# Attention, the last group of four heads: all four scores of a turn in one round, in seven PSUM banks

## The chip, the cores and the metric

The kernel runs on one core of a Trainium2 chip. The metric is the device time of one execution in microseconds (us), and the time of a kernel is the median of its runs. A core has engines that run side by side, each through its own list of instructions in order: PE (TensorE, matrix products), ACT (ScalarE), DVE (VectorE), POOL (GpSimd), and SP, which here only issues DMAs. Semaphores tie them together. PE writes its products into PSUM, eight banks of 128 partitions by 512 float32; ACT and DVE read them from there.

## What is computed

The program is a network of eight layers over x, 4 batches of 1024 tokens by 128 features in float32, each layer adding to x a function of the layer norm of x. Two of the eight are softmax attention, and both are written by one function, so that the change is in both. Cut to what matters:

```python
# L2: 8 heads of 16 features
scores = einsum('bhsd,bhtd->bhst', q, k) / sqrt(dk)
att    = einsum('bhst,bhtd->bhsd', softmax(scores), v)

# L3: 16 heads of 8 features, keys in blocks of 64
exp_scores = exp(scores - m_new)
l_new   = chunk_sum * corr + chunk_sum
out_new = out * corr + einsum('bhqk,bhkd->bhqd', exp_scores, V_blk)
...       # at the end out / l
```

For each head the kernel finds the largest score of each query (the maxima), then the exponentials of the scores less that maximum, then their product with the values.

## The kernel before, in words

`attention` (line 1116) works through groups of four heads of one batch: M = 8 groups in L2 and 16 in L3. The four heads of a group lie on partitions 0, 32, 64 and 96 of a q and a k tile, so that a product over one head's features takes 32 rows of PE's array, and the four heads have four different strips of rows.

The outer loop (line 1397) counts turns, 16 for a group. In turn t one group is scanned (its maxima are found) while the group before it is weighed (its exponentials are taken). A turn has two rounds:

- `scan` (line 1254) takes a PSUM tile of two banks, tag "pa", from a ring of two such tiles: four banks in all. `score` (line 1263) writes two heads' scores into it with two matmuls (line 1265), and one reduction on DVE takes both heads' maxima (line 1273 or 1277).
- `weigh` (line 1310) is called twice in a round, for one head each time: it takes one bank, tag "sm", from a ring of three, writes the head's scores of 128 keys by 512 queries with one matmul (line 1319), and one exponential on ACT (line 1323) reads the bank and writes a quarter of the SBUF tile es.
- `gather` (line 1325) multiplies es with the values: four matmuls (line 1341), one for each head, each taking 32 columns of the array, into the one bank of tag "po". It runs over half of the 512 queries at a time: in round 0 of turn t the second half of turn t-2, in round 1 the first half of turn t-1. Where a new stretch of 512 queries begins (each eighth turn), the first half is passed over and the next round does all 512 columns; after eight turns DVE copies the bank out (line 1348).
- Other steps hang on a turn and round through `at` (line 1353) and are emitted behind the round's own work: `negate` (line 1224), which turns the maxima over and sends them through DRAM into a row of q, `spread`, `value` and `project`, which prepare the next group or batch, and `collect` (line 1356) with the steps of `finish`.

The schedule is written by hand (line 1178): each engine gets its instructions in the order in which the loop emits them. A PSUM tile that is taken anew can be written once all that used its slot before is done.

In the first group there is only scanning (`scan_alone`, line 1281). In the last group there is only weighing: turns M*16 to M*16+15. There the loop before still emits two rounds: heads 2 and 3, a gather, heads 0 and 1, a gather. The "pa" tiles aren't used there: no later group is scanned or projected, and the steps of `finish` that take one come before this stretch or behind it. `negate` of the last group's second half of queries falls into round 1 of its first turn, `collect` of the group before into its second, and the layer norm's sums of three batches (`ln_sums`, line 128, on DVE) into its fourth, seventh and tenth.

Of the kernel before, what the change touches and what calls it, by code (L numbers as in the profile page):

```python
# [9 lines left out]
F32 = mybir.dt.float32  # L10
AF = mybir.ActivationFunctionType
# [4 lines left out]
P = 128  # L16
# [11 lines left out]
class Net:  # L28
# [1087 lines left out]
    def attention(self, H, HD, scale, weights, prepare, finish, last=False):  # L1116
# [13 lines left out]
        nc, tc = self.nc, self.tc  # L1130
        G = H // 4
        W = 32 * H
        M = NB * G
        TURNS = 2 * TPB
        NBM = 9 if last else 2
        wq, wk, wv = weights
        with ExitStack() as c:
# [4 lines left out]
            sm = c.enter_context(tc.tile_pool(name="ats", bufs=3, space=PSUM))  # L1142
# [8 lines left out]
                cp, lhsT=ones.rearrange("p a b -> p (a b)"), rhs=self.ones[0:1, 0:1], start=True, stop=True  # L1151
# [28 lines left out]
            def pair(name):  # L1180
                return pap.tile([P, 2, 512], F32, tag="pa", name=name).rearrange("p a b -> p (a b)")
# [72 lines left out]
            def scan(m, turn, hp):  # L1254


                st = state[m]
                i, n = turn // 2, turn % 2
                if "bm" not in st:
                    st["bm"] = [two.tile([P, 4, 4, NBM], F32, tag=f"bm{h}", name=f"bm{h}") for h in range(2)]  # L1260
                pa = pair("pa").rearrange("p (a b) -> p a b", a=2)

                def score(j):
                    r = slice(32 * j, 32 * j + 32)
                    nc.tensor.matmul(  # L1265
                        pa[:, j % 2, :], lhsT=st["q"][r, i * P : (i + 1) * P],
                        rhs=st["k"][r, n * 512 : (n + 1) * 512], start=True, stop=True,
                    )

                def reduce():  # L1270
                    out = st["bm"][i // 4][:, i % 4, 2 * hp : 2 * hp + 2, :]
                    if last and n == 1:
                        nc.vector.tensor_reduce(  # L1273
                            out[:, :, 1:9], pa.rearrange("p j (c s) -> p j c s", c=8), axis=AX.X, op=ALU.max
                        )
                    else:
                        nc.vector.tensor_reduce(out[:, :, n : n + 1], pa, axis=AX.X, op=ALU.max)  # L1277

                return score, reduce

            def scan_alone(m, turn):


                st = state[m]
                i, n = turn // 2, turn % 2
                if n == 0:
                    both = [scan(m, turn, hp) for hp in range(2)]
                    for j in range(4):
                        both[j // 2][0](j)
                    for _, reduce in both:  # L1290
                        reduce()
                    return
                banks = [sm.tile([P, 512], F32, tag="sm", name="pb") for _ in range(3)]
                banks.append(pop.tile([P, 512], F32, tag="po", name="pb"))
                for j in range(4):
                    r = slice(32 * j, 32 * j + 32)
                    nc.tensor.matmul(
                        banks[j], lhsT=st["q"][r, i * P : (i + 1) * P],
                        rhs=st["k"][r, n * 512 : (n + 1) * 512], start=True, stop=True,
                    )  # L1300
                for j in range(4):
                    out = st["bm"][i // 4][:, i % 4, j, :]
                    if last:
                        nc.vector.tensor_reduce(  # L1304
                            out[:, 1:9], banks[j].rearrange("p (c s) -> p c s", c=8), axis=AX.X, op=ALU.max
                        )
                    else:
                        nc.vector.tensor_reduce(out[:, n : n + 1], banks[j], axis=AX.X, op=ALU.max)  # L1308

            def weigh(m, turn, j):  # L1310

                st = state[m]
                n, kc = turn // TPB, turn % TPB
                es = st.setdefault("es", {})
                if turn not in es:
                    es[turn] = two.tile([P, 4, 512], F32, tag="es", name="es", bufs=5)
                pb = sm.tile([P, 512], F32, tag="sm", name="pb")
                r = slice(32 * j, 32 * j + 32)
                nc.tensor.matmul(  # L1319
                    pb, lhsT=st["k"][r, kc * P : (kc + 1) * P], rhs=st["q"][r, n * 512 : (n + 1) * 512],  # L1320
                    start=True, stop=True,
                )
                nc.scalar.activation(es[turn][:, j, :], pb, AF.Exp, scale=scale)  # L1323

            def gather(m, turn, half):


                st = state[m]
                b, g = m // G, m % G
                n, kc = turn // TPB, turn % TPB  # L1330
                if kc == 0:
                    if half == 0:
                        return
                    st["po"] = pop.tile([P, 512], F32, tag="po", name="po")
                    if n == 0:
                        st["oT"] = two.tile([P, SEQ], F32, tag="oT", name="oT")
                es, po = st["es"][turn], st["po"]
                cols = slice(0, 512) if kc == 0 else slice(256 * half, 256 * half + 256)
                for j in range(4):
                    r = slice(32 * j, 32 * j + 32)  # L1340
                    nc.tensor.matmul(  # L1341
                        po[r, cols], lhsT=vring[b % 2][:, kc, 4 * g + j, :], rhs=es[:, j, cols],
                        start=kc == 0, stop=True, skip_group_check=True,
                    )
                if half == 1:
                    del st["es"][turn]
                    if kc == TPB - 1:
                        nc.vector.tensor_copy(st["oT"][:, n * 512 : (n + 1) * 512], po)  # L1348
# [22 lines left out]
            for b in range(NB):  # L1371

                t = b * G * TURNS
# [5 lines left out]
            for m in range(M):  # L1379
                t = m * TURNS  # L1380
# [15 lines left out]
            t = 0  # L1396
            while t < (M + 1) * TURNS or jobs:
                scans, weighs = TURNS <= t < M * TURNS, TURNS <= t < (M + 1) * TURNS
                if t < TURNS:
                    scan_alone(0, t)  # L1400
                for rnd in range(2):

                    other = 2 - 2 * rnd
                    if scans:
                        score, reduce = scan(t // TURNS, t % TURNS, rnd)
                    if weighs:
                        weigh(t // TURNS - 1, t % TURNS, other)
                    if scans:
                        for j in range(2):
                            score(2 * rnd + j)  # L1410
                        reduce()
                    if weighs:
                        weigh(t // TURNS - 1, t % TURNS, other + 1)

                    w, half = (t - 2, 1) if rnd == 0 else (t - 1, 0)
                    if TURNS <= w < (M + 1) * TURNS:
                        gather(w // TURNS - 1, w % TURNS, half)
                    for what, args in jobs.pop((t, rnd), ()):
                        what(*args)
                t += 1  # L1420
# [405 lines left out]
```

## Time and profile before

| | us |
|---|---|
| median of 3 runs | 2668.34 |
| lowest and highest of the 3 | 2666.43, 2669.78 |
| the profiled execution | 2665.29 |
| its span in the trace | 2663.6 |
| PE busy | 2417.5 (91% of the span) |
| DVE busy | 1795.2 (67%) |
| ACT busy | 1501.7 (56%) |
| first and last exponential of line 1323 | 1014.1, 2529.6 |

The trace of one execution gives each instruction's start and length on its engine. "Busy" of PE says that matmuls are in flight, not that the array works at its peak. A float32 matmul has two records of PE in this trace: line 1319 has 3072 records for 1536 exponentials. "PEld" is the load of the stationary operand, which goes ahead of the matmul. "Idle before" an instruction is the time in which its engine had nothing to do, with what ended it. The chain of waits is followed back from the last instruction: each step is what released the next. PEclk is the share of PE's clock pulses that the chip granted.

### The profile page before, as it was taken

What the parts mean: (1) busy time and instruction counts of PE and PEld (TensorE: products, weight loads), DVE (VectorE), ACT (ScalarE), POOL (GpSimd) and SP (SyncE); (2) the same over time, 40 slices, a digit from 0 to 9 for tenths busy, and PEclk for the clock granted to TensorE, in tenths of its full rate; (3) what the DMA queues carried; (4) which work ended last, traced back from release to release, by engine and by line L of the source; (5) the groups of instructions that cost most, each with busy time, mean ns of one, the idle gap of its engine ahead of it and who ended that gap; (6) DMA issues with size and microseconds to landing.
All of it is one profiled execution on the core that took longest, in us unless ns stands there. A gap on an engine that the chain in (4) does not pass through costs nothing.

```text
span 2663.6 us, 51041 instructions
## 1 busy us (share of the span) xinstructions
PE 2417.5 (91%) x19913; PEld 1222.1 (46%) x19913; DVE 1795.2 (67%) x3670; ACT 1501.7 (56%) x3333; POOL 293.0 (11%) x525
## 2 busy tenths in 40 slices
PE   5687758899997979999999779999999999999968
PEld 3455535699995333333333443333333333333356
DVE  5888877476764767776774357767767776777233
ACT  4466468455554434665566635666666566666632
POOL 6012021000002530000000440000000000000011
PEclk8699879899997989999999879999999999999969
DMA  1333320000000001001000000000000000000000
GB/s 45 74 77 74 73 74 1 1 1 1 1 1 2 1 9 18 14 15 18 14 14 6 5 5 10 9 10 8 8 9 12 8 9 10 8 8 8 3 18 18
DMA packets 116719, 46.66 MB, mean 18 GB/s; under 512 B 88473, under 2 KB 111097, under 8 KB 116474
## 3 DMA queue, kind: packets, MB, share of 16 engines
q1 hardware_dynamic: 116474, 43.35, 8.2%
q8 instruction: 159, 2.61, 0.4%
q14 instruction: 86, 0.70, 0.1%
HBM read 17.04 MB, written 12.98 MB: 11 GB/s over the span
## 4 chain that ended last, share of the span: by engine, by line
PE 57%; DVE 4%; ACT 1%; POOL 1%; issue 1%; SPq 0%; DMA 0%; POOLq 0%; DVEq 0%; ACTq 0%
PE pb L1319 32%; PE po L1341 16%; PE pa L1265 2%; DVE bm L1277 1%; PE pp L1205 1%; PE pv L1186 1%; DVE bm L1304 1%; PE tp L158 1%; PE gp L1014 1%; PE rp L1743 1%; DVE bm L1308 0%; PE pr L1598 0%; PE rp L1520 0%; PE ph L1756 0%; POOL sg L1753 0%
## 5 line engine op out<-in xcount | busy, mean ns | idle before, releaser
L1323 ACT ACTIVATE es<-pb 128x512 f32<-128x512 f32 x1536 | 836.3, 594 | 536.1 <-PE pb L1319 381.8
L1319 PE MATMUL pb<-q,k 32*128 32x512 f32 x3072 | 956.5, 641 | 3.9 <-DVE bm L1308 1.7
L1265 PE MATMUL pa<-k,q 32*128 32x512 f32 x2944 | 846.0, 650 | 10.4 <-DMA q<-q 10.3
L1277 DVE TENSOR_REDUCE bm<-pa 128x2 f32<-128x1024 f32 x496 | 605.0, 1225 | 261.1 <-PE pb L1319 168.0
L1341 PE MATMUL po<-es,v 128*32 128x256 f32 (+1 forms) x5760 | 480.0, 405 | 0.0
L1319 PEld LDWEIGHTS pb<-q,k 32*128 32x128 f32 x3072 | 313.5, 183 | 350.7 <-ACT es L1323 189.8
L1341 PEld LDWEIGHTS po<-es,v 128*32 128x32 f32 x5760 | 114.2, 108 | 543.1 <-issue 508.2
L1273 DVE TENSOR_REDUCE bm<-pa 128x16 f32<-128x1024 f32 x240 | 293.2, 1222 | 97.3 <-PE pb L1319 60.7
L1265 PEld LDWEIGHTS pa<-k,q 32*128 32x128 f32 x2944 | 234.4, 186 | 37.0 <-issue 18.6
L152 POOL TENSOR_SCALAR xn<-x,rs,nm 128x128 f32<-128x128 f32 x112 | 50.3, 464 | 1204.6 <-DVE nm L125 1026.9
L366 DVE TENSOR_TENSOR pr<-T,L 128x31 f32<-128x31 f32 (+15 forms) x248 | 92.0, 371 | 28.0 <-DMA L<-ld 20.7
L369 DVE TENSOR_TENSOR T<-T,pr 128x31 f32<-128x31 f32 (+15 forms) x248 | 93.1, 375 | 8.5
L1348 DVE COPY oT<-po 128x512 f32<-128x512 f32 x48 | 32.8, 682 | 95.6 <-PE po L1341 95.6
L158 PE MATMUL tp<-ident,xn 128*128 128x128 f32 x224 | 47.0, 361 | 42.7 <-ACT xn L154 38.1
L821 ACT ACTIVATE w<-tr,half 128x128 f32<-128x128 f32 x128 | 47.1, 368 | 48.3 <-PE tr L819 45.6
L796 ACT ACTIVATE a<-hp,wb 128x128 f32<-128x128 f32 x128 | 47.1, 368 | 41.6 <-PE hp L792 40.1
L1081 PE MATMUL ep<-L_ffn_expert_w,xnT 128*128 128x512 f32 x128 | 66.8, 654 | 3.3 <-DVE x L1090 3.1
L324 PE MATMUL wide<-bt,kt 32*128 32x128 f32 x512 | 29.9, 360 | 43.9 <-DVE mt L413 31.7
L486 PE MATMUL sp<-ux,kn 128*128 128x256 f32 x128 | 46.1, 493 | 17.7 <-ACT ux L475 17.7
L158 PEld LDWEIGHTS tp<-ident,xn 128*128 128x128 f32 x224 | 33.9, 179 | 61.2 <-ACT xn L154 47.0
L804 DVE TENSOR_TENSOR dlt<-gr,mask 128x128 f32<-128x128 f32 x96 | 28.0, 292 | 48.3 <-PE gr L802 48.3
L853 ACT COPY dr<-tr 128x128 f32<-128x128 f32 x128 | 34.1, 266 | 43.1 <-PE tr L851 41.1
(466 smaller groups left out, 3598.8 us busy)
## 6 DMA issues: line engine op xcount, KB each, us to landing
ld<-kk SPq DMA_DIRECT2D x128, 32.0 KB
L<-ld SPq DMA_DIRECT2D x8, 512.0 KB
td<-T SPq DMA_DIRECT2D x8, 512.0 KB
tb<-td SPq DMA_DIRECT2D x128, 32.0 KB
md<-nt SPq DMA_DIRECT2D x192, 2.0 KB
q<-md SPq DMA_DIRECT2D x192, 2.0 KB
x<-in_L_attn_x_dram SPq DMA_DIRECT2D x4, 512.0 KB
od<-o SPq DMA_DIRECT2D x32, 64.0 KB
```

The costliest lines, as they stand in the source:

```text
L152: nc.gpsimd.tensor_scalar(xn[:, i, :], src[:, i, :], sl, bl, ALU.mult, ALU.add)
L158: nc.tensor.transpose(tp[:, i, :], xn[:, 4 * n + i, :], self.ident)
L366: nc.vector.tensor_mul(pv, T[:, 0 : j + 1, j : j + 1].to_broadcast(sh), L[:, j : j + 1, j + 1 :].to_broadcast(sh))
L369: nc.vector.tensor_sub(T[:, 0 : j + 1, j + 1 :], T[:, 0 : j + 1, j + 1 :], pv)
L796: nc.scalar.activation(self.a, self.hp, AF.Silu, bias=B1)
L1081: nc.tensor.matmul(ep.rearrange("p a b -> p (a b)"), lhsT=self.tok(t), rhs=ew[:, 4 * h : 4 * h + 4, :].rearrange("p a b -> p (a b)"), star ...
L1265: nc.tensor.matmul(pa[:, j % 2, :], lhsT=st["q"][r, i * P : (i + 1) * P], rhs=st["k"][r, n * 512 : (n + 1) * 512], start=True, stop=True,)
L1273: nc.vector.tensor_reduce(out[:, :, 1:9], pa.rearrange("p j (c s) -> p j c s", c=8), axis=AX.X, op=ALU.max)
L1277: nc.vector.tensor_reduce(out[:, :, n : n + 1], pa, axis=AX.X, op=ALU.max)
L1319: nc.tensor.matmul(pb, lhsT=st["k"][r, kc * P : (kc + 1) * P], rhs=st["q"][r, n * 512 : (n + 1) * 512], start=True, stop=True,)
L1323: nc.scalar.activation(es[turn][:, j, :], pb, AF.Exp, scale=scale)
L1341: nc.tensor.matmul(po[r, cols], lhsT=vring[b % 2][:, kc, 4 * g + j, :], rhs=es[:, j, cols], start=kc == 0, stop=True, skip_group_check=True,)
```

## The change

`weigh` takes a list of heads and a function that gives it banks. It takes all banks of the list, then emits the matmuls of all heads, then their exponentials. While a group is scanned, it is called as before: one head, a bank of tag "sm". In the last group it is called once in a turn, in round 0, for all four heads, and round 1 has only its gather and the steps that hang on it. The banks come there from `any_bank`: whenever its list is empty it takes two "pa" tiles, which give two banks each, and three "sm" banks, and it hands these seven out in that order.

```diff
-            def weigh(m, turn, j):
+            def weigh(m, turn, js, bank):
...
-                pb = sm.tile([P, 512], F32, tag="sm", name="pb")
-                r = slice(32 * j, 32 * j + 32)
-                nc.tensor.matmul(
-                    pb, lhsT=st["k"][r, kc * P : (kc + 1) * P], rhs=st["q"][r, n * 512 : (n + 1) * 512],
-                    start=True, stop=True,
-                )
-                nc.scalar.activation(es[turn][:, j, :], pb, AF.Exp, scale=scale)
+                pbs = [bank() for _ in js]
+                for j, pb in zip(js, pbs):
+                    r = slice(32 * j, 32 * j + 32)
+                    nc.tensor.matmul(
+                        pb, lhsT=st["k"][r, kc * P : (kc + 1) * P], rhs=st["q"][r, n * 512 : (n + 1) * 512],
+                        start=True, stop=True,
+                    )
+                for j, pb in zip(js, pbs):
+                    nc.scalar.activation(es[turn][:, j, :], pb, AF.Exp, scale=scale)
+
+            def bank():
+                return sm.tile([P, 512], F32, tag="sm", name="pb")
+
+            spare = []
+
+            def any_bank():
+
+                if not spare:
+                    for _ in range(2):
+                        pa = pair("pe")
+                        spare.extend(pa[:, i * 512 : i * 512 + 512] for i in range(2))
+                    spare.extend(bank() for _ in range(3))
+                return spare.pop(0)
...
-                    if weighs:
-                        weigh(t // TURNS - 1, t % TURNS, other)
+                    if weighs and scans:
+                        weigh(t // TURNS - 1, t % TURNS, (other,), bank)
+                    elif weighs and rnd == 0:
+                        weigh(M - 1, t % TURNS, range(4), any_bank)
...
-                    if weighs:
-                        weigh(t // TURNS - 1, t % TURNS, other + 1)
+                    if weighs and scans:
+                        weigh(t // TURNS - 1, t % TURNS, (other + 1,), bank)
```

## The prediction

> **What bounds the kernel now.** I read first the chain of waits, by line. It names PE, and PE in attention:
>
> ```profile
> PE pb L1319 32%; PE po L1341 16%; PE pa L1265 2%; DVE bm L1277 1%; PE pp L1205 1%; PE pv L1186 1%; DVE bm L1304 1%; PE tp L158 1%; PE gp L1014 1%; PE rp L1743 1%; DVE bm L1308 0%; PE pr L1598 0%; PE rp L1520 0%; PE ph L1756 0%; POOL sg L1753 0%
> ```
>
> Only the last group changes, so I read that stretch alone. The chain in order of time, L3 (start, length, what):
>
> ```profile
> 2473.42 0.57 PE po L1341 x8
> 2473.99 1.22 PE pb L1319 x4
> 2475.20 0.57 PE po L1341 x8
> 2475.77 1.07 PE pb L1319 x4
> 2476.84 0.57 PE po L1341 x8
> ...
> 2480.31 0.59 ACT es L1323
> ...
> 2482.06 1.00 PE po L1341 x8
> 2483.05 1.06 PE pb L1319 x4
> ```
>
> The reader is to see that nothing but PE stands there: scores of two heads (1.07 or 1.22), a gather (0.57), over and over. Two rounds make a turn of 3.43 us. The gather that begins a stretch of 512 queries does 512 columns and takes 1.00, so 256 columns more cost 0.43 and 0.14 of each gather is fixed (changing from row strips to column strips and back). The 1.22 rounds are those in which the second head's bank was released late. L2's stretch shows the same numbers.
>
> Then the last full round of scanning just before, in the timeline (start, length, engine, line, what):
>
> ```profile
> 2472.28 0.69 PE L1319 MATMUL pb<-q,k 32*128 32x512 f32 x1
> 2472.28 0.70 PE L1265 MATMUL pa<-k,q 32*128 32x512 f32 x2
> 2472.30 1.10 PE L1319 MATMUL pb<-q,k 32*128 32x512 f32 x2
> ...
> 2472.82 0.59 PE L1265 MATMUL pa<-k,q 32*128 32x512 f32 x2
> 2472.83 0.59 PE L1319 MATMUL pb<-q,k 32*128 32x512 f32 x1
> ...
> 2473.35 0.64 PE L1341 MATMUL po<-es,v 128*32 128x256 f32 x8
> 2473.43 1.08 ACT L1323 ACTIVATE es<-pb 128x512 f32<-128x512 f32 x2 [0.70 <-PE pb L1319]
> 2473.52 1.23 DVE L1273 TENSOR_REDUCE bm<-pa 128x16 f32<-128x1024 f32 x1 [0.56 <-PE pb L1319]
> ...
> 2480.29 1.57 ACT L1323 ACTIVATE es<-pb 128x512 f32<-128x512 f32 x3 [0.70 <-PE pb L1319]
> ```
>
> Four heads, one on each strip of rows, begin at 2472.28 and the gather follows at 2473.35: 1.07 us, what two heads cost in the last group. Their exponentials begin 1.15 after the scores. The last group thus uses half of the array's strips in the same time. The same stretch by windows:
>
> ```profile
> 2474.00:2529.00 55.00, 54.63 (x360) 17.06 (x360) 9.51 (x46) 34.28 (x65) 0.00 (x0) 1.00 0.03 4
> ```
>
> PE is busy for 54.63 of 55 us, DVE 9.51, ACT 34.28, with the clock granted in full: ACT has a third of the time free.
>
> **The change, part by part.** The stretch runs from the first score of the last group (2473.92) to the copy of the last product (2531.39): 57.47 us. In L2 it is 1423.77 to 1481.24, 57.47 too. No instruction is added or removed: 64 score matmuls, 64 exponentials and all gathers stay; they move.
>
> *A turn on PE.* Scores of four heads once: 1.06. Two gathers in a row: their columns equal those of the 512-column gather, 1.00. Sum 2.06 instead of 3.43. Is PE's list fast enough? A turn issues 24 weight loads with their matmuls. At the end of the stretch 14 loads pass in 0.58 us, so 24 need 1.0; covered.
>
> *A turn on ACT.* Three exponentials in 1.57 with one at 0.60: the next starts 0.485 after the one before. Four: 1.94 a turn, 0.12 under PE. Here the Trainium skill speaks against the change: "TensorEngine Tiling (Array Packing)", section PSUM Bottleneck, says that tiling speeds up the matmuls but not the emptying of PSUM, which may then bound. And "ScalarE: Activation LUTs", section What ACT_TABLE_LOAD costs, prices an ACTIVATE with immediates at 186 ns + 0.833 ns an element and lets neighbours overlap by 93 ns: 612 - 93 = 519 ns each, estimated 2.08 a turn, so that ACT would bound by 0.02. The row gives 0.485, and I take it; by the page the total would be some 0.8 us worse over both layers. Either way the two engines nearly meet: little more is to be had from PE here. From above, with no overlap, an exponential costs 0.60 and the turn 2.40 (a rival below).
>
> *Does PE wait for ACT?* The gather of turn t-1 stands behind the scores of turn t and needs the exponentials of t-1. Those end 1.15 + 3 x 0.485 + 0.60 = 3.21 after their scores began, so 1.15 after the scores of t began; the gather comes at 1.06 + 0.43 = 1.49. No wait, 0.3 to spare.
>
> *Banks.* Seven banks, four a turn: the fourth head of a turn takes a bank used one turn before. If it is an "sm" bank, its exponential was the first of that turn and ended at 1.15 + 0.60 = 1.75, plus 0.06 (the trace's step from an exponential's end to the next load on PE): before 2.06. If it opens a "pa" tile, I take it that both halves must be read first; where these are the first two heads of the turn before, that is 0.485 later, 2.29, and the head starts 0.23 late. Counting the order of the seven through 16 turns gives four such turns, and two of 0.18 behind a turn with one gather less: 1.3 us. Queued behind a late head are the gathers, so it counts in full.
>
> *First turn.* Its third head takes the "pa" tile that DVE's last reduction reads until 2474.75, 0.89 with the 0.06 after 2473.92. This wait is new, and before nothing stood there. Turn 0: 0.89 + 2.06 = 2.95. `negate` hangs on DVE and keeps its place.
>
> *The end.* From the last scores: 3.21 to the end of the exponentials, 0.06, then both halves' products to the copy, 1.12 (the last chain before ran 2530.27 to 2531.39): 4.39.
>
> *Sum.* 2.95 + 14 x 2.06 + 1.3 + 4.39 = 37.5 us instead of 57.5: 20.0 us for each layer, 40.0 for both.
>
> *What was hidden and might show.* The DVE copy of the group before: before, it ended 1.40 after its gather began (2478.56 to 2479.96), and the next gather into that bank now comes 0.57 + 1.06 = 1.63 after; covered by 0.2, and with the cover gone it costs that difference twice in a layer. The maxima of the second half reach q through SP: the last issue ends at 2480.74, and turn 8 begins at 2473.92 + 2.95 + 7 x 2.06 = 2491.3; the longest q transfer on the chain is 2.33, so covered by 8. `ln_sums` and `negate`: DVE works 9.5 us of 37. The work behind the stretch (output DMAs on SP, transposes, layer norm) hangs on the last copy and shifts whole. SP is past the earlier DMAs at 2486 and idle until the end.
>
> *Against the time.* The profiled execution took 2665.3 (span 2663.6); less 40.0 it is 2625.3. The median of the runs is 3.0 above it, so I forecast 2628.
>
> **The rivals.**
>
> - *The two halves of a "pa" tile are tied together*: the matmul into the second half waits until the first half has been read. Within a turn this costs nothing, as all four matmuls precede the exponentials. Four times in 16 turns a tile straddles two turns, and then the next scores wait for all exponentials: 3.27 instead of 2.06, 1.2 each, 4.8 a layer: 2638. For: no row shows a tile read half by half. Against: they are separate banks, and the two score matmuls of one tile show no wait for each other. Chance 0.08.
> - *ACT becomes the bound*: exponentials in a long row at 0.60, a turn of 2.40. 0.34 x 15, less the bank waits it swallows, plus 0.35 at the end: 4.1 a layer, 2636. For: the skill's page, halfway. Against: 1.57 for three. Chance 0.06.
> - *The four don't run side by side*: two pairs, 2.12 + 1.00 = 3.12 a turn, 0.31 x 15 + 0.7 at the end saved: 2658. Against: the scan round, with the same strips, shapes and banks of the same two tags. Chance 0.03.
> - *The other side: the clock.* A turn streams 1.72 us and has 0.34 fixed; at a granted clock c it takes 1.72/c + 0.34, and passes 3.43 below c = 0.56. At 0.50, which windows from 2539 on show behind the attention, the turn is 3.78, the stretch 63.7 and the kernel 2681. For: PE's clock does fall there. Against: it falls where PE was idle for 5 us, and scanning with four strips has 1.00. Waits can't do it: even if scores waited for all exponentials of the turn before, a turn would be 3.27, still under 3.43. Chance 0.03.
>
> **How the numbers follow.** The forecast has 0.78; around it, 0.1 us a turn either way is 3 us for both layers, and runs of one kernel differ by 3.4. The range 2620 to 2638 takes in the first two rivals, and leaves out the third, the fourth and mishaps. From no change I can tell 0.2%, 5.3 us: all but the clock are faster by more. Faster 0.95, same 0.02, slower 0.03.
>
> **What would show it.** In the changed trace's last group: eight score records starting together on four strips, about 1.06 before the gather; 16 gather matmuls in a row; turns of 2.06, of which six last some 0.2 longer; ACT busy for over nine tenths; the stretch 37.5 long in both layers. I am wrong if score rounds stay at two a turn, if PE waits for ACT at each turn, if the exponentials' spacing is over 0.5, or if PEclk falls there.

## The result, and the profile after

| | before | changed |
|---|---|---|
| median of the runs, us | 2669.06 (4 runs) | 2637.38 (4 runs, 2633.47 to 2647.7) |
| ratio to before, 95% interval | | 0.989 [0.9868, 0.9911] |
| the stretch of the last group in L2, us | 57.47 | 42.00 |
| the same in L3 | 57.47 | 42.00 |

The stretch is, as in the prediction, from the last group's first score to its last copy: 1424.76 to 1466.76 in L2, 2459.94 to 2501.94 in L3. It gained 15.5 us a layer where 20.0 were forecast; 30.9 in both, and the medians differ by 31.7.

The profiled execution has a span of 2638.0, only 25.6 under that of before. The other 5.3 us are not in the two stretches: 3.9 of them lie behind the last copy, the rest ahead of the two. Behind the copy the same work met another clock. By windows, first a row of before, then the same part of the changed kernel (stretch, length, PE, PEld, DVE, ACT and POOL busy, PEclk, DMA share, GB/s):

```profile
2601.40:2621.40 20.00, 17.52 (x132) 13.88 (x131) 10.97 (x19) 6.03 (x13) 3.34 (x5) 0.97 0.10 27
```

```profile
2571.90:2591.90 20.00, 17.99 (x104) 13.77 (x103) 10.21 (x17) 4.74 (x10) 2.87 (x4) 0.72 0.10 27
```

At 0.72 PE got through 104 matmuls in the 20 us in which it did 132 at 0.97. From the last copy to the end it is 136.1 us here and 132.2 before; in the traces of the runs below it is anything from 130.5 to 136.0. So I compare stretches, and medians over runs, not spans of two traces.

The chain of waits in L3's last group, in order of time, as shown of before (start, length, what):

```profile
2460.01 1.94 PE pe L1320 x8
2461.95 1.00 PE po L1357 x16
2462.95 0.64 PE pb L1320 x3
...
2464.10 2.07 ACT es L1325 x4
2466.17 0.04 issue
2466.22 0.70 PE pe L1320 x3
...
2467.36 1.43 PE po L1357 x16
2468.78 0.63 PE pb L1320 x2
...
2472.02 4.13 ACT es L1325 x8
2476.15 0.04 issue
2476.19 0.69 PE pe L1320
...
2477.33 1.00 PE po L1357 x16
2478.33 1.14 PE pe L1320 x8
...
2479.50 4.13 ACT es L1325 x8
2483.63 0.04 issue
2483.67 0.69 PE pe L1320
```

What was forecast is there: one score round a turn, both gathers in one row of 16 matmuls (1.00), the first turn's wait (1.94 for the scores, the turn 2.94), four exponentials in 2.07. What is new: ACT stands on the chain. Before the scores of turns 2, 6 and 9 (and 13, behind this cut) PE waits until every exponential of the turn before is done: the last ends at 2466.17 and the scores start at 2466.22. Each time the matmul that waits writes a "pe" bank, a half of a "pa" tile. The windows say the same in sum:

```profile
2462.90:2499.00 36.10, 31.73 (x336) 11.40 (x336) 7.91 (x41) 29.51 (x59) 0.00 (x0) 1.00 0.04 6
```

PE is busy for 31.73 of 36.10 us at the full clock; it stands still for 4.4, and ACT isn't full either. Where the wait sits can be read from the built program's list of PE's instructions (shortened), with the semaphore that each waits for:

```
L1320 Matmult pb_25995<-q0,k0 128x512
L1320 Matmult pb_25996<-q0,k0 128x512
L1320 Matmult pb_25997<-q0,k0 128x512
L1320 Matmult pe_26030<-q0,k0 128x512 [waits Activation]
L1357 Matmult po_25828<-es_25964,v1 32x256 x4
L1320 Matmult pe_26030<-q0,k0 128x512 [waits Activation]
```

This is turn 1 and the start of turn 2. The tile pe_26030 is shared: its first half goes to the last head of turn 1, its second half to the first head of turn 2. The second half is a bank that nobody has used since the tile was taken, yet its matmul waits for ACT. The count that it waits for is the one that the exponential of turn 1's last head raises, the reader of the first half. The built program puts the tile into banks 0 and 1, so the two halves share no bank. (The matmul into the first half waits as forecast, for both exponentials that read the tile's place before.)

### The profile page after: what moved, and what is told of

It reads as the page before. It is cut to its first block, busy times and chain, and to the rows that moved or that the text cites. A ratio compares the mean times of both kernels' runs of the same rounds, so it can differ in the third digit from the quotient of the medians.

```text
span 2638.0 us, 51055 instructions
## 1 busy us (share of the span) xinstructions
PE 2384.1 (90%) x19913; PEld 1216.0 (46%) x19913; DVE 1793.4 (68%) x3670; ACT 1497.1 (57%) x3333; POOL 291.6 (11%) x525
## 4 chain that ended last, share of the span: by engine, by line
PE 55%; DVE 4%; ACT 2%; POOL 1%; issue 1%; SPq 0%; DMA 0%; POOLq 0%; DVEq 0%; ACTq 0%
PE pb L1320 30%; PE po L1357 16%; PE pa L1265 2%; DVE bm L1277 1%; ACT es L1325 1%; PE pp L1205 1%; PE pe L1320 1%; DVE bm L1304 1%; PE pv L1186 1%; PE tp L158 1%; PE rp L1762 1%; PE gp L1014 1%; DVE bm L1308 0%; PE pr L1617 0%; PE kp L1530 0%
## 5 line engine op out<-in xcount | busy, mean ns | idle before, releaser
L1325 ACT ACTIVATE es<-pb 128x512 f32<-128x512 f32 x1462 | 795.7, 595 | 496.1 <-PE pb L1320 339.3
L1320 PE MATMUL pb<-q,k 32*128 32x512 f32 x2924 | 905.8, 640 | 3.2 <-DVE bm L1308 1.7
L1320 PEld LDWEIGHTS pb<-q,k 32*128 32x128 f32 x2924 | 295.3, 183 | 325.7 <-ACT es L1325 170.4
L324 PE MATMUL wide<-bt,kt 32*128 32x128 f32 x512 | 30.4, 365 | 43.0 <-DVE mt L413 30.9
```

The lines of the kernel that those rows point to most:

```text
L1320: nc.tensor.matmul(pb, lhsT=st["k"][r, kc * P : (kc + 1) * P], rhs=st["q"][r, n * 512 : (n + 1) * 512], start=True, stop=True,)
```

## The experiments

Two theories. **Tie**: the program treats a "pa" tile as one thing, so that a matmul into its second half waits until the first half has been read; four turns of 16 begin with such a half. **Supply**: seven banks are too few for four a turn, with ACT this full, whichever way they are dealt out. Each experiment computes the whole function. The edits of the first and of the last experiment are shown against the changed kernel, those of the three between them against the first. The runs of before with which the first four are compared have a median of 2666.31.

**No tile shared by two turns.** The same banks, two "sm" and one whole "pa" tile a turn:

```diff
                 if not spare:
-                    for _ in range(2):
-                        pa = pair("pe")
-                        spare.extend(pa[:, i * 512 : i * 512 + 512] for i in range(2))
-                    spare.extend(bank() for _ in range(3))
+                    spare.extend(bank() for _ in range(2))
+                    pa = pair("pe")
+                    spare.extend(pa[:, i * 512 : i * 512 + 512] for i in range(2))
```

> The same change, the same seven banks, but each turn takes two 'sm' banks for heads 0 and 1 and one whole 'pa' tile for heads 2 and 3, so that no 'pa' tile is shared by two turns. Tie theory (a matmul into the second half of a 'pa' tile waits until the first half has been read): the stalls before the scores of turns 2, 6, 9 and 13 go (1.7 + 3 x 0.98 = 4.6 us a layer), as do the late fourth heads and most of the wait in the first turn; the last group's stretch, first score to last copy, takes 35.7 us a layer instead of 42.0, and the kernel some 2625. Supply theory (seven banks are too few for four a turn with ACT this full, whichever way they are dealt out): the stretch stays at 42 or above, the kernel at 2637.

Measured: 2625.45 (2616.14 to 2626.08, 5 runs), ratio to before 0.9834 [0.9808, 0.986]; the stretch 36.19 us in both layers. The chain in its L3 stretch, and a window of it:

```profile
2467.67 0.63 PE pb L1320 x2
2468.30 0.01 PE pe L1320 x2
2468.31 0.41 PE pb L1320 x2
2468.72 0.01 PE pe L1320 x2
2468.74 1.00 PE po L1356 x16
2469.74 0.63 PE pb L1320 x2
```

```profile
2454.00:2486.00 32.00, 32.00 (x357) 11.19 (x360) 8.29 (x44) 31.04 (x62) 0.00 (x0) 1.00 0.04 7
```

ACT is off the chain, a turn is 2.07 (2467.67 to 2469.74), PE is busy throughout and ACT for 31.04 of 32. No bank was added. Supply falls.

**The tie in every turn.** The same deal, one head later:

```diff
-            spare = []
+            spare, spares = [], []
...
-                    spare.extend(bank() for _ in range(2))
+                    spare.extend(bank() for _ in range(2 if spares else 3))
                     pa = pair("pe")
                     spare.extend(pa[:, i * 512 : i * 512 + 512] for i in range(2))
+                    spares.append(1)
```

> As e1_aligned, but dealt out one head later: the first turn takes three 'sm' banks and the first half of a 'pa' tile, and from then on each turn begins with the second half of the tile of the turn before, then two 'sm' banks, then the first half of the next tile. Banks, matmuls and exponentials are those of e1_aligned, only every turn now shares a tile with the next. Tie theory: every turn waits for all exponentials of the turn before, 3.27 us a turn, the stretch 53 us a layer, the kernel some 2660. Supply theory: no different from e1_aligned; with late heads by bank alone the stretch would be 38 us.

Measured: 2659.86 (20 runs), ratio 0.9974 [0.9966, 0.9983]; the stretch 53.5 us. The chain, L3:

```profile
2474.54 2.05 ACT es L1325 x4
2476.60 0.04 issue
2476.64 0.69 PE pe L1320
...
2477.82 2.06 ACT es L1325 x4
2479.87 0.04 issue
2479.92 0.69 PE pe L1320
```

PE and ACT take turns: a turn is 3.28 (2476.64 to 2479.92), 3.27 by the sum. Between this kernel and the one before it nothing differs but the head at which the deal begins, and that is 17 us a layer. This is the strongest evidence for the tie: the same instructions, the same banks.

**The order within a turn.** No tile is shared, but the tile goes first:

```diff
-                    spare.extend(bank() for _ in range(2))
                     pa = pair("pe")
                     spare.extend(pa[:, i * 512 : i * 512 + 512] for i in range(2))
+                    spare.extend(bank() for _ in range(2))
```

> As e1_aligned, no tile shared between turns, but the 'pa' tile goes to heads 0 and 1 and the 'sm' banks to heads 2 and 3. What a bank waits for is then a later exponential: the fourth head takes the 'sm' bank that the third head had a turn before, read as the third of four, 1.15 + 2 x 0.485 + 0.60 + 0.06 = 2.78 after the scores began, 0.7 later than a turn of 2.06. Tie theory with release by order: every other turn 2.77, the stretch 41 us a layer, the kernel some 2636, though no tile straddles. Supply theory: the same as e1_aligned.

Measured: 2637.87 (4 runs), ratio 0.9884 [0.9857, 0.9911]; the stretch 41.9 us, just what the changed kernel takes, for another reason. The chain, L3:

```profile
2470.47 0.63 PE pe L1320 x2
2471.10 0.01 PE pb L1320
2471.11 0.42 PE pe L1320 x2
2471.53 0.78 PE pb L1320 x3
2472.31 1.00 PE po L1356 x16
2473.31 0.63 PE pe L1320 x2
...
2475.39 0.63 PE pe L1320 x2
```

Here the last head's "pb" comes 0.78 late every other turn: 2.84 and 2.08 us a turn (2470.47, 2473.31, 2475.39). A bank comes free in the order in which its exponential stands among the four: with the same banks and no tile shared, the order alone costs 5.7 us a layer (41.9 against 36.19).

**Two heads at a time with enough banks.** The loop of before, on the banks of the first experiment:

```diff
-                    elif weighs and rnd == 0:
-                        weigh(M - 1, t % TURNS, range(4), any_bank)
+                    elif weighs:
+                        weigh(M - 1, t % TURNS, (other, other + 1), any_bank)
```

> The loop of before in the last group, two rounds a turn with two heads and a gather each, but with the banks of e1_aligned: 'sm' banks in round 0, a 'pa' tile in round 1. It takes away the late second heads (rounds of 1.22 become 1.06) and keeps the two heads at a time and the four switches between score and gather. Theory that the gain lies in four heads side by side and one switch to and from the gathers: a turn of 3.26, the stretch 54 us a layer (57.5 before), the kernel some 2662. Theory that the gain lies in the banks alone: the stretch near 36 to 42.

Measured: 2654.81 (20 runs), ratio 0.9954 [0.9943, 0.9966]; the stretch 52.1 us. The chain, L3:

```profile
2474.26 1.06 PE pb L1320 x4
2475.32 0.57 PE po L1356 x8
2475.89 0.63 PE pe L1320 x2
2476.51 0.23 PE pb L1320 x2
2476.75 0.19 PE pe L1320 x2
2476.94 0.23 PE pb L1320 x2
2477.18 1.00 PE po L1356 x8
```

This is 5.4 us a layer less than before. I had forecast 54 and 2662: in turns 1 and 9 one round has no gather, and then the scores of four heads stand together in the list and run side by side from 2475.89, which my sum did not count. They take 1.29 there (to 2477.18), where in the kernel before the same scores took 2.86 (2479.20 to 2482.06), waiting for a bank that ACT read:

```profile
2479.20 1.11 PE pb L1319 x4
2480.31 0.59 ACT es L1323
2480.90 0.04 issue
2480.94 1.12 PE pb L1319 x2
```

Twice 1.57 is 3.1 of the 5.4. The other 2.3 are the late second heads, which are gone in every round but the first (1.06 instead of 1.22). The remaining 15.9 us down to the first experiment's 36.19 are four heads at a time and half of the switches to and from the gathers, taken together. Banks alone are not the gain.

**Four banks, and the direct comparison.** The changed kernel again, the first experiment again on the same chip, and a version that takes only the two "pa" tiles, whole, each turn:

```diff
-                    for _ in range(2):
-                        pa = pair("pe")
-                        spare.extend(pa[:, i * 512 : i * 512 + 512] for i in range(2))
-                    spare.extend(bank() for _ in range(3))
+                    pa = pair("pe")
+                    spare.extend(pa[:, i * 512 : i * 512 + 512] for i in range(2))
```

> The changed kernel once more, unaltered, on one chip with r_aligned. Both theories: as before, 42.0 us a layer for the stretch, and 31 us under the kernel before (2 x 15.5).

> e1_aligned once more, on one chip with r_after. Tie theory: the stretch 36.2 us a layer as in e1_aligned, 2 x 5.8 = 11.6 us under r_after. If the difference between e1_aligned and the changed kernel came from the chip or from the clock behind the attention, it goes.

> The changed kernel with four banks instead of seven in the last group: each turn takes both 'pa' tiles, whole, and no 'sm' bank. No tile is shared by two turns. Tie theory with release by order: heads 0 and 1 wait until the second exponential of the turn before is done (2.29 after its scores began), heads 2 and 3 until the fourth; ACT takes up part of this, and the stretch is 45 us a layer, the kernel some 2643: three banks are worth less than 10 us a layer, and four banks without a straddle lose only 3.5 us a layer to seven with four straddles. Supply theory: with four banks scores and exponentials take turns, 3.27 us a turn, the stretch 53 or more, the kernel above 2659.

Measured, against 2669.78 before on this chip: the changed kernel 2638.39, ratio 0.989 [0.9874, 0.9905]; the first experiment 2625.76, ratio 0.9836 [0.982, 0.9851]; four banks 2647.61, ratio 0.9921 [0.9903, 0.9938]. Stretches 42.00, 36.19 and 46.1 us. The first two repeat: 12.6 us apart by the medians, 11.6 by the stretches. Four banks are 1 us a layer dearer than forecast, and 7 us cheaper than seven with the tie in every turn. The chain of the version with four banks, L3:

```profile
2471.19 1.14 PE pe L1320 x8
2472.33 0.02 issue
2472.36 1.09 ACT es L1325 x2
2473.45 0.04 issue
2473.49 2.11 PE pe L1320 x8
2475.60 1.00 PE po L1355 x16
```

The next scores start when two exponentials are done (2473.45), not four: a tile that is taken anew waits for its own two readers.

The first experiment is the better version: with its deal of the banks the kernel is 41 to 44 us under before in the two comparisons, and it beats the changed kernel too.

## Why the prediction was off

The kernel got faster, as forecast, by the mechanism that was forecast; but the time lies 9 us above the 2628 given, where the first rival stood (2638). That is also the upper end of the range: by the median the result lies just inside it, by its ratio to the runs of before (0.989, where 2638 / 2668.34 is 0.9886) just beyond. The step that failed is **Banks**. It says: "If it opens a 'pa' tile, I take it that both halves must be read first", and from this it counted only when a tile is *taken*. It took its second half to be free once the tile is, and came to 1.3 us a layer. The rival that ties the halves together had 0.08, because "they are separate banks, and the two score matmuls of one tile show no wait for each other". Both are true and neither bears on it: before, no "pa" tile is read by half, so these tiles could not show the case.

"No row shows a tile read half by half" is true of attention only. In an earlier layer the tile "wide" (line 316), of four banks, is used in two parts: matmuls into columns 0 to 255 of each bank, which ACT reads (line 348), and into columns 256 to 511, which DVE reads (line 413). The trace of before has this (start, length, engine, line, what):

```profile
136.68 1.22 DVE L413 TENSOR_TENSOR mt<-wide,upper 128x1024 f32<-128x1024 f32 x1
138.05 0.73 PE L324 MATMUL wide<-bt,kt 32*128 32x128 f32 x16 [1.01 <-DVE mt L413]
```

These matmuls write the part that ACT reads, and they start when DVE has read the other (at 137.90); PE was idle for 1.01 us before them. The profile has twelve such waits, 31.7 us in sum. The two parts share their banks, so this can't tell a tracking by tile from one by bank. But it shows that a write into one part can wait for the reader of another, and the rival deserved more than 0.08.

Term by term, L3, from the starts of the turns in the changed trace (turn 15's scores at 2497.51, from 2459.94):

| step | forecast | measured |
|---|---|---|
| turn 0, with the wait for DVE's last reduction | 2.95 | 2.94 |
| 14 turns without waits for banks | 28.8 | 29.0 |
| waits for banks | 1.3 | 5.7 |
| from the last scores to the copy | 4.39 | 4.4 |
| the stretch | 37.5 | 42.0 |

The waits: 1.70 before turn 2 and 0.98 before each of turns 6, 9 and 13, the four places that the rival counted (4.6 in sum, 4.8 by its own working); and late fourth heads of about 0.28 in three turns where I had 0.23, and 0.16 in turn 10.

The other steps held. *A turn on PE*: 2.07, forecast 2.06, with no limit from the list of instructions; two gathers in a row take 1.00, apart they took 2 x 0.57. *A turn on ACT*: four exponentials in 2.06 to 2.07, which is 3 spacings of 0.485 and 0.60. The Trainium skill's figures ("ScalarE: Activation LUTs", What ACT_TABLE_LOAD costs), 612 ns and a spacing of 519, would have made an estimated 2.17. By its own pace ACT bounds no turn, but in the first experiment it is at 31.04 of 32: the warning in "TensorEngine Tiling (Array Packing)", section PSUM Bottleneck, is right about what follows, not about this change. One reading was too short: in the chain of before "nothing but PE" is not quite so, for the row shown at 2480.31 is ACT's, where PE waits for a late bank. *The gathers* do not wait for ACT. *The hidden work* stayed hidden. *The clock* is 1.00 throughout the stretch. The sum without the tie, 37.5, is not shown with the deal of the changed kernel: no run frees its halves from each other and keeps their order. The first experiment's 36.19 has another deal, with fewer late heads, and comes close to what the same arithmetic gives it (35.7).

## What to carry to other kernels

When a buffer of several banks is handed out in parts, ask at which grain the program tracks it: here a part that was free waited for the reader of its neighbour, and where such a pair spans two steps, two engines that should overlap take turns. Deal the parts so that a buffer lives and dies within one step: here 5.8 us a layer (42.00 to 36.19) with no bank more. And let the banks that the next step needs soonest be read first: here 5.7 us (41.9 to 36.19). A case that the changed stretch does not show before the change, such as a first read by halves, deserves more than a small chance, and a look for something like it elsewhere in the trace.

## What the runs showed of the hardware

Four matmuls on four strips of rows that stand together in PE's list cost what two do, where no bank is late: 1.07 in the first experiment (2467.67 to 2468.74), 1.06 for two heads. Where they come from two rounds, in the version with two heads at a time, they took 1.29 (2475.89 to 2477.18), with two of them late.

The part outside the change differs more from trace to trace than I had allowed: from the last copy to the end it took 130.5 to 136.1 us, in two traces of the changed kernel 136.1 and 134.6, and the stretch of one kernel, the first experiment's, began in L2 at 1423.01 in one trace and at 1428.67 in the other. The stretch itself came out the same to 0.01 us in both layers and in both traces.
